# Layer 3's scores with both batches on the partitions, and every weighted sum over 256 columns in quarters

## The chip, the cores and the metric

The kernel runs on one core of one Trainium2 chip. The metric is the device time of one execution in microseconds. Most executions agree within 0.3%.

## What is computed

Four graph layers run on `x`, 32 batches of 512 nodes with 64 features, over one graph `adj` of 512 x 512. Each layer takes `h = max(layernorm(x), 0)` and adds its result to `x`.

```python
# layer 0: three steps of  v = W2 relu(W1 [v, adj v] + b1) + b2
# layer 1: two steps of    z = relu((adj z) W_i)
# layer 2: 8 heads and then one output head of
s = einsum('bnd,bmd->bnm', h, h) * graph
s = where(s == 0.0, -1e16, s)
a = softmax(s, axis=2)
out = einsum('bnm,bmd->bnd', a, h) + b          # h = x @ W
# layer 3: adj with ones on its diagonal
h = x @ weight
e = leaky_relu((h @ a[:D])[:, :, None] + (h @ a[D:])[:, None, :], 0.2)
h_prime = einsum('bij,bjd->bid', softmax(adj * e), h)
return h_prime + bias
```

So each pair of batches needs 16 score matrices of layer 2's heads, two of its output head and two of layer 3, all of 512 x 512 in float32.

## The kernel before

Batches go in 16 pairs, the two batches of a pair side by side. A *unit* is a set of scores in a tile `sm` of 128 partitions x 8 slots x 512 columns, taken from a ring of three such tiles. There are ten units for a pair: eight heads (`Heads`, each with 512 nodes in two parts of 64 partitions), the output head (`Out`), which holds 64 nodes of batch 0 in partitions 0 to 63 and 64 nodes of batch 1 in the others, and layer 3 (`Last`). In `Last` before, slots 0 to 3 belong to batch 0 and slots 4 to 7 to batch 1, with 128 nodes on the partitions.

A unit goes through steps. `scores` makes two slots at a time: TensorE for heads and `Out` (line 422, and line 425 adds the mask), and for `Last` one product for each batch of a repeated vector with the features `h3T` (line 690) and then ScalarE's Prelu with the source term `src` as bias (line 692). `maxima` multiplies a slot by the graph and takes its maximum on VectorE (line 443); the negated maxima are made on GpSimd (line 450). `exponentials` is ScalarE (line 454), `normalise` is a reciprocal on VectorE (line 464) and the scaling on GpSimd (line 466), `turn` transposes blocks of 32 x 32 on VectorE (line 472).

After the turn, the weighted sum over neighbours runs on TensorE in tiles of 32 rows x 64 columns. For each of 16 blocks of neighbours (`jb`) it takes products of the node features in quarters (`vq`) with the turned scores. A sum of two heads (`Two`, line 482) has eight products of 256 columns in a block, in both halves of the array's columns. `Ends` (line 750) sums the output head of one pair together with layer 3 of the pair before it: four products of 256 columns for the first, and eight of 128 columns for the second, four for each batch. The last three sums of the program, one of `Out` and two of `Last`, stand alone. Each float32 product shows as two instructions.

A sum lies in the four banks of the tag `mm`; the scores have four banks of their own, of the tag `s`. `evict` copies a finished sum to SBUF, to a tile of the tag `us`, of which there are two. For heads, line 516 reads it, and line 527 writes the activated result `y`; for `Ends`, lines 769 and 771 write it and line 588 turns it.

`quarters` (line 288) spreads node features over four groups of 32 partitions with 16 DMAs on SP's queue. It is called for the heads' values (`z`, two batches), the output head's (`hn`) and layer 3's (`h3n`, both batches in a row, line 671). `Out.chain` makes layer 3's inputs: `oA`, `oB`, `oC` are the layer norm, `oT` the transposed features, `oW` the product with the weight (line 649), `oN` the node features and source terms (lines 660, 668 and 669) and their quarters.

The order of all this on the engines is written out by hand. A step is a job with a tick and a place in it (`PLACES`); there are ten ticks a pair, and one sorted list of jobs gives the order of the instructions on each engine's queue. The letters are: `s` scores, `r` maxima, `x` exponentials, `n` normalise, `t` turn, `v` the parts of a weighted sum, `us` or `eu` the eviction, `w` and `y` the heads' weights, `o` and `c` the projection, `f` and `h` the output head's features and nodes, `F0` to `F24` the steps of layers 0 and 1 for the next pair. The units of the last stretch have an order of their own, `TAIL`. A sum is placed in two halves, `vA` and `vB`.

Of the kernel before, what the change touches and what calls it, by code (L numbers as in the profile page):

```python
# [21 lines left out]
def gnn_stack_kernel(  # L22
# [79 lines left out]
    A = const.tile([P, NT, N], F32, name="A")  # L102
# [3 lines left out]
    ones = const.tile([P, P], F32, name="ones")  # L106
    ivt = const.tile([1, 2, D], F32, name="ivt")
    W1n = const.tile([P, 2, P], F32, name="W1n")
    W2n = const.tile([P, P], F32, name="W2n")
# [8 lines left out]
    rows = const.tile([NB, P], F32, name="rows")  # L118
# [31 lines left out]
    nc.sync.dma_start(out=Wo_sb, in_=W_out.rearrange("(h d) o -> d h o", d=HID))  # L150

# [6 lines left out]
    b2rep = const.tile([P, P], F32, name="b2rep")  # L158
# [8 lines left out]
    A3 = A  # L167
    a2rep = const.tile([P, 2, P], F32, name="a2rep")
# [35 lines left out]
    def masks():  # L204

        for k in range(2):
            nc.vector.tensor_tensor(II[:, k, :], ident[:, 0:D], ident[:, D:P], ALU.add)
        nc.vector.tensor_copy(I2b, II[:, 0, :])

        nc.vector.tensor_scalar(NEGM, A, 0.0, NEG_INF, ALU.is_equal, ALU.mult)  # L210

        for t in range(NT):
            nc.gpsimd.affine_select(
                out=A3[:, t, blk(t)],
                in_=A[:, t, blk(t)],
                pattern=[[-1, P]],
                compare_op=ALU.not_equal,
                fill=1.0,
                base=0,
                channel_multiplier=1,  # L220
            )
# [5 lines left out]
    def grams():  # L227

        WT = hp.tile([P, H, D], F32, tag="us", name="WT")
# [10 lines left out]
    def vectors():  # L240
        for j in range(2):
            nc.vector.tensor_scalar(a2rep[:, j, :], ones, a2bd[:, j : j + 1], None, ALU.mult)
# [3 lines left out]
        w3T = hp.tile([P, P], F32, tag="us", name="w3T")  # L246
# [158 lines left out]
    class Unit:  # L405
# [68 lines left out]
        def weigh(self, part):  # L474
# [3 lines left out]
            for jb in range(part * JB // 2, (part + 1) * JB // 2):  # L478
# [21 lines left out]
    class Two(Unit):  # L500
# [30 lines left out]
        def stages(self):  # L531

            def evict():
                self.us = hp.tile([P, 4, N // 2], F32, tag="us", name="us")
# [36 lines left out]
            def nodes():  # L571
                s = state[self.p]
                pn = turned(s["HH"][self.j])
                hn = hp.tile([P, NT, D], F32, tag="hn", bufs=1, name="hn")
# [15 lines left out]

    def to_nodes(yT):
        return turned(yT).rearrange("p (t j d) -> p t j d", t=NT, j=2)

    class Out(Unit):
# [12 lines left out]
        def stages(self):  # L607
            s = state[self.p]

            def evict():  # L610

                self.yT = hp.tile([P, N], F32, tag="us", name="yT")
# [21 lines left out]
        def chain(self):  # L634
# [18 lines left out]
            def nodes():  # L653
                s["h3n"] = hp.tile([P, NT, 2, D], F32, tag="h3n", bufs=1, name="h3n")
                s["src"] = st.tile([P, NT, 2], F32, tag="src", name="src")
                for c in range(2):
# [12 lines left out]
                    nc.vector.tensor_copy(s["src"][:, 2 * c : 2 * c + 2], pn[:, :, P:])  # L669
# [8 lines left out]
    class Last(Unit):  # L678
# [5 lines left out]
        def scores(self, k):  # L684
            s = state[self.p]
            j = k // 2
            if k == 0:
                self.pd = [ps_s.tile([P, N], F32, tag="s", name="pd") for _ in range(2)]
                for pd, r, n in zip(self.pd, R, range(2)):
                    nc.tensor.matmul(pd, lhsT=a2rep[r, n, :], rhs=s["h3T"][r, :], start=True, stop=True)  # L690
            for i in range(2 * k, 2 * k + 2):
                nc.scalar.activation(
                    self.sm[:, i, :], self.pd[j], AF.Prelu, bias=s["src"][:, i % NT, j : j + 1], alpha=0.2
                )

        def maxima(self, i):
            self.by_graph(i, self.sm[:, i, :], A3[:, i % NT, :])
# [3 lines left out]
        def weighed(self, i, c):  # L701
            return state[self.p]["h3Q"][c], self.sm[:, c * NT : (c + 1) * NT, :]

        def stages(self):
            s = state[self.p]

            def evict():
                self.yT = hp.tile([P, N], F32, tag="us", name="yT")
                yT = self.yT.rearrange("p (t k i e) -> p k i t e", k=2, i=2, e=32)
                for i in range(4):  # L710
                    nc.scalar.activation(
                        yT[:, i // 2, i % 2],
                        self.u[i][:, 0:P].rearrange("p (t e) -> p t e", e=32),
# [4 lines left out]
            def residual():  # L718
                pn = to_nodes(self.yT)
                xo = xp.tile([P, NT, 2, D], F32, tag="xo", bufs=1, name="xo")  # L720
                nc.vector.tensor_tensor(xo, pn, s["x3"], ALU.add)
                for j in range(2):
                    nc.sync.dma_start(
# [6 lines left out]
    class Ends(Unit):  # L730
# [6 lines left out]


        def weigh(self, part):
            if part == 0:  # L740
                self.u = [mm_ps() for _ in range(4)]
            for jb in range(part * JB // 2, (part + 1) * JB // 2):
# [298 lines left out]
```

## Time and profile before

| | |
|---|---|
| median of 3 runs | 2349.54 us (2346.86 to 2351.03) |
| the profiled execution | 2346.53 us |
| its span, first to last instruction | 2344.7 us |
| mean granted TensorE clock | 0.977 |
| ScalarE's exponentials, line 454 | 912.2 us busy, 1280 of them |
| GpSimd's scaling, line 466 | 882.6 us busy, 1280 |
| VectorE's transposes, line 472 | 776.6 us busy, 640 |
| VectorE's maxima of heads and `Out`, line 443 | 733.0 us busy, 1152 |
| TensorE's sums of two heads, line 482 | 488.1 us busy |
| TensorE's joint sums, line 750 | 131.4 us busy |

Busy times of TensorE are unions over instructions that run side by side in several tiles of the array. "Idle before" in a row is the time for which the engine had nothing to run just ahead of the instruction, with what ended it behind the arrow. SPq is the queue on which SP issues DMAs, PEld TensorE's weight loads.

### The profile page before, as it was taken

Reading aid. Unit: us, or ns where it says so; the run is one execution under the profiler, and the core shown is the slowest. Engines: PE = TensorE matmul, PEld = TensorE weight load, DVE = VectorE, ACT = ScalarE, POOL = GpSimd, SP = SyncE. Lnnn points to the kernel's source line nnn. Section 1 sums busy time; section 2 is a strip of 40 time slices with the busy share of each in tenths; the row PEclk is TensorE's granted clock in tenths of the full one; section 3 lists DMA queues with packets and bytes.
Section 4 is the critical chain, followed back from the end, with each engine's and each line's share of the span. In section 5 each row is a group of like instructions: output and inputs, shape, how many; then the busy total and the mean of one; then the engine's idle time right before and its main releaser. Section 6 shows DMA issues by size and latency. Waiting matters only on the chain.

```text
span 2344.7 us, 81823 instructions
## 1 busy us (share of the span) xinstructions
PE 2189.2 (93%) x34507; PEld 1186.5 (51%) x34507; DVE 1872.8 (80%) x4098; ACT 1496.4 (64%) x3752; POOL 1306.7 (56%) x2163
## 2 busy tenths in 40 slices
PE   6889999999999999999999999999999999999883
PEld 3335555555555555555555555555555555554452
DVE  3558788888887888888888888888888888888654
ACT  1346557667676766767676676767667676766644
POOL 2345465655665565566656556665655666555433
PEclk9899999999999999999999999999999999999986
DMA  3001111202121120212112021211202121120112
GB/s 85 10 15 20 24 20 24 42 13 40 20 41 25 22 43 13 40 20 41 25 25 42 12 40 21 41 25 24 42 13 40 20 36 25 24 38 13 28 25 46
DMA packets 260596, 68.25 MB, mean 29 GB/s; under 512 B 257660, under 2 KB 258692, under 8 KB 260228
## 3 DMA queue, kind: packets, MB, share of 16 engines
q1 hardware_dynamic: 259424, 62.86, 15.9%
q8 instruction: 270, 4.42, 0.8%
q14 instruction: 98, 0.80, 0.1%
q10 hardware_dynamic: 804, 0.17, 0.0%
HBM read 8.40 MB, written 4.19 MB: 5 GB/s over the span
## 4 chain that ended last, share of the span: by engine, by line
PE 76%; DVE 10%; ACT 6%; POOL 3%; issue 2%; SPq 2%; DMA 1%; ACTq 0%; POOLq 0%; DVEq 0%
PE s L422 19%; PE mm L482 16%; PE mm L312 11%; PE mm L750 5%; PE mm L545 5%; PE s L425 4%; PE mm L516 4%; DVE sm L443 4%; DVE sm L472 4%; ACT sm L454 3%; PE mm L324 3%; PE mm L798 2%; SPq L294 2%; PE mm L358 2%; ACT y L527 1%
## 5 line engine op out<-in xcount | busy, mean ns | idle before, releaser
L454 ACT ACTIVATE sm<-sm,nmx 128x512 f32<-128x512 f32 x1280 | 912.2, 720 | 204.9 <-POOL nmx L450 198.0
L466 POOL TENSOR_SCALAR sm<-sm,rs 128x512 f32<-128x512 f32 x1280 | 882.6, 707 | 183.8 <-DVE rs L464 173.9
L472 DVE STREAM_TRANSPOSE sm<-sm 128x1024 f32<-128x1024 f32 x640 | 776.6, 1229 | 99.3 <-POOL sm L466 94.4
L443 DVE CUSTOM_DVE_ANT_0 sm<-s,A 128x512 f32<-128x512 f32 x1152 | 733.0, 680 | 139.1 <-PE s L425 131.7
L422 PE MATMUL s<-ZZ,Y 64*64 64x512 f32 x4096 | 572.0, 604 | 20.7 <-DVE mx L443 13.2
L482 PE MATMUL mm<-sm,vq 32*64 32x256 f32 (+1 forms) x17152 | 488.1, 378 | 29.8 <-DVE sm L472 20.3
L450 POOL TENSOR_SCALAR nmx<-mx 128x2 f32<-128x2 f32 x640 | 143.0, 229 | 608.5 <-DVE mx L443 550.8
L482 PEld LDWEIGHTS mm<-sm,vq 32*64 32x64 f32 x17152 | 400.3, 135 | 129.3 <-issue 56.6
L422 PEld LDWEIGHTS s<-ZZ,Y 64*64 64x64 f32 x4096 | 149.9, 132 | 254.0 <-issue 124.8
L425 PE MATMUL s<-NEGM,I2b 64*64 64x512 bf16 x2304 | 259.4, 378 | 0.0
L454 ACT ACTIVATION_READ_ACCUMULATOR sm<-sm,nmx 128x1 f32 x1280 | 250.1, 195 | 0.0
L537 ACT COPY us<-mm 128x256 f32<-128x256 f32 x256 | 75.9, 380 | 182.5 <-PE mm L482 182.5
L312 PE MATMUL mm<-AT,v 128*128 128x512 f32 x384 | 172.9, 593 | 0.0
L527 ACT ACTIVATE y<-mm,cols 128x512 f32<-128x512 f32 x256 | 159.9, 686 | 9.1 <-PE mm L516 9.1
L425 PEld LDWEIGHTS <-I2b 64*64 64x64 bf16 x2304 | 81.1, 107 | 160.5 <-issue 160.4
L750 PE MATMUL mm<-sm,vq 32*64 32x128 f32 (+1 forms) x5504 | 131.4, 313 | 27.4 <-issue 21.5
L516 PE MATMUL mm<-us,Wh 64*64 64x512 f32 x1024 | 134.1, 595 | 17.4 <-ACT us L537 17.4
L272 POOL TENSOR_TENSOR r<-ve,mhalf 128x8 f32<-128x8 f32 x64 | 110.8, 1731 | 54.4 <-DVE ve L270 39.4
L750 PEld LDWEIGHTS mm<-sm,vq 32*64 32x64 f32 x5504 | 111.8, 132 | 52.7 <-issue 29.4
L263 POOL TENSOR_TENSOR xc<-x,nmu 128x512 f32<-128x512 f32 x48 | 55.3, 1151 | 139.8 <-DVE nmu L261 139.8
L545 PE MATMUL mm<-y,Wo_sb 128*64 128x512 f32 x512 | 125.2, 605 | 0.0
L312 PE MATMUL mm<-AT,z 128*128 128x512 f32 x256 | 119.1, 609 | 3.8 <-DVE z L276 1.4
(135 smaller groups left out, 1979.0 us busy)
## 6 DMA issues: line engine op xcount, KB each, us to landing
vq<-z SPq DMA_DIRECT2D x512, 32.0 KB, 1.9
vq<-hn SPq DMA_DIRECT2D x512, 32.0 KB, 1.9
vq<-h3n SPq DMA_DIRECT2D x512, 32.0 KB, 1.9
xt<-in_x_dram SPq DMA_DIRECT2D x32, 128.0 KB, 2.4
out_dram<-xo SPq DMA_DIRECT2D x32, 128.0 KB, 2.0
A<-in_adj_dram SPq DMA_DIRECT2D x3, 1024.0 KB
Wh<-in_L_gnn_Wh_dram SPq DMA_DIRECT2D x2, 256.0 KB
Wo_sb<-in_L_gnn_W_out_dram SPq DMA_DIRECT2D x1, 256.0 KB
```

The costliest lines, as they stand in the source:

```text
L312: nc.tensor.matmul(pe, lhsT=v[:, m].rearrange("p j d -> p (j d)"), rhs=AT[:, m, :], start=(first and m == 0), stop=(m == NT - 1),)
L422: nc.tensor.matmul(pss[half][R[ab], :], lhsT=lhsT, rhs=rhs, start=True, stop=False)
L425: nc.tensor.matmul(pss[half][R[ab], :], lhsT=I2b[R[half], :], rhs=NEGM[R[half], k, :], start=False, stop=True,)
L443: nc.vector.tensor_tensor_reduce(self.sm[:, s, :], src, graph, 1.0, -FMAX, ALU.mult, ALU.max, self.mx[:, s : s + 1])
L454: nc.scalar.activation(self.sm[:, s, :], self.sm[:, s, :], AF.Exp, bias=self.nmx[:, s : s + 1], accum_out=self.ssum[:, s : s + 1],)
L466: nc.gpsimd.tensor_scalar(self.sm[:, s, :], self.sm[:, s, :], self.rs[:, s : s + 1], 1.0, ALU.mult, ALU.mult)
L472: nc.vector.transpose(out=two, in_=two)
L482: nc.tensor.matmul(self.u[i][R[c], 0 : weights.shape[1] * 32], lhsT=values[32 * i : 32 * i + 32, jb, :], rhs=weights[32 * i : 32 * i + 32, ...
L516: nc.tensor.matmul(py[c][r, :], lhsT=Wh2[R[c], 2 * (self.q - 1 + c) + ab, r], rhs=self.us[R[c], 2 * ab : 2 * ab + 2].rearrange("p i (s e) ...
L527: nc.scalar.activation(y, py[c], AF.Prelu, bias=cols[:, h : h + 1], alpha=0.01)
L545: nc.tensor.matmul(pa[R[ab], :], lhsT=Wo_sb[:, h, :], rhs=self.y[h], start=(k == 0), stop=(k == 1),)
L750: nc.tensor.matmul(self.u[i][R[c], (s % NS) * 32 : (s + ns) * 32], lhsT=values(i)[r, jb, :], rhs=sm[r, s : s + ns, 32 * jb : 32 * jb + 32] ...
```

## The change

Layer 3's unit takes the form of the output head's: a slot has 64 nodes, of batch 0 on partitions 0 to 63 and of batch 1 on the others. One product makes its scores for both batches. The graph for it, `A3`, is a tile of its own with 64 nodes twice on the partitions, loaded from `adj` by two more DMAs of 1 MB and given ones on its diagonal by 16 selections in the first pair. The source terms, which line 669 leaves with 128 nodes on the partitions, are moved to the new form by four DMAs in a pair. The joint sum has 256 columns in each product. All sums are placed in four quarters, `vA` to `vD`. The tag `us` has one buffer, `hn` and `h3n` share one, and tiles that only the start needs (`A`, `W1n`, `W2n`, `ones`, `rows`, `b2rep`) lie in the places of later ones. `PLACES` and `TAIL` are new throughout.

```diff
-    A = const.tile([P, NT, N], F32, name="A")
+    A = ap_.tile([P, NT, N], F32, tag="sm", name="A")
+    A3 = const.tile([P, NS, N], F32, name="A3")
...
-    ones = const.tile([P, P], F32, name="ones")
-    W1n = const.tile([P, 2, P], F32, name="W1n")
-    W2n = const.tile([P, P], F32, name="W2n")
+    early1 = hp.tile([P, 4, P], F32, tag="h3T", bufs=1, name="early1")
+    W1n, W2n, ones = early1[:, 0:2], early1[:, 2], early1[:, 3]
+    early2 = hp.tile([P, 2, P], F32, tag="h3n", bufs=1, name="early2")
...
     nc.sync.dma_start(out=Wo_sb, in_=W_out.rearrange("(h d) o -> d h o", d=HID))
+    for r in R:
+        nc.sync.dma_start(out=A3[r], in_=adj.rearrange("(s q) m -> q s m", q=D))
...
-        for t in range(NT):
-            nc.gpsimd.affine_select(
-                out=A3[:, t, blk(t)],
...
+    def loops():
+        for s in range(NS):
+            for base in (0, -D):
+                nc.gpsimd.affine_select(
+                    out=A3[:, s, hblk(s)],
+                    in_=A3[:, s, hblk(s)],
...
         def weigh(self, part):
-            for jb in range(part * JB // 2, (part + 1) * JB // 2):
+            for jb in range(part * JB // 4, (part + 1) * JB // 4):
...
-                self.us = hp.tile([P, 4, N // 2], F32, tag="us", name="us")
+                self.us = hp.tile([P, 4, N // 2], F32, tag="us", bufs=1, name="us")
...
-                hn = hp.tile([P, NT, D], F32, tag="hn", bufs=1, name="hn")
+                hn = hp.tile([P, NT, D], F32, tag="h3n", bufs=1, name="hn")
...
-                    nc.vector.tensor_copy(s["src"][:, 2 * c : 2 * c + 2], pn[:, :, P:])
+                    nc.vector.tensor_copy(src[:, 2 * c : 2 * c + 2], pn[:, :, P:])
+                s["src"] = st.tile([P, NS], F32, tag="src", bufs=2, name="src")
+                for j in range(2):
+                    for h in range(2):
+                        nc.sync.dma_start(
+                            out=s["src"][R[j]].rearrange("r (t h) -> r t h", h=2)[:, :, h], in_=src[R[h], :, j]
+                        )
                 tag = "h3Q" if self.p < NPAIR - 1 else "hQ"
                 s["h3Q"] = [quarters(s["h3n"][:, :, j, :], f"{tag}{j}") for j in range(2)]
...
             if k == 0:
-                self.pd = [ps_s.tile([P, N], F32, tag="s", name="pd") for _ in range(2)]
-                for pd, r, n in zip(self.pd, R, range(2)):
-                    nc.tensor.matmul(pd, lhsT=a2rep[r, n, :], rhs=s["h3T"][r, :], start=True, stop=True)
+                self.pd = ps_s.tile([P, N], F32, tag="s", name="pd")
+                nc.tensor.matmul(self.pd, lhsT=a2rep, rhs=s["h3T"], start=True, stop=True)
...
     class Ends(Unit):
         def weigh(self, part):
-            for jb in range(part * JB // 2, (part + 1) * JB // 2):
-                tiles = [(0, 0, NS, lambda i: state[self.attn.p]["hQ"][i // 2], self.attn.sm)]
-                if self.last:
-                    for j in range(2):
-                        tiles.append((1, j * NT, NT, lambda i, j=j: state[self.last.p]["h3Q"][j], self.last.sm))
...
+            units = [(state[self.attn.p]["hQ"], self.attn.sm)]
+            if self.last:
+                units.append((state[self.last.p]["h3Q"], self.last.sm))
+            for jb in range(part * JB // 4, (part + 1) * JB // 4):
+                for (values, sm), r in zip(units, R):
                     for i in range(4):
+                        q = slice(32 * i, 32 * i + 32)
                         nc.tensor.matmul(
+                            self.u[i][r, 0 : N // 2],
+                            lhsT=values[i // 2][q, jb, :],
+                            rhs=sm[q, :, 32 * jb : 32 * jb + 32],
+                            start=(jb == 0),
+                            stop=(jb == JB - 1),
                         )
...
-        for part, half in enumerate("AB"):
-            at(t, f"v{half}{k}", lambda part=part: unit.weigh(part))
+        for part, quarter in enumerate("ABCD"):
+            at(t, f"v{quarter}{k}", lambda part=part: unit.weigh(part))
...
+        if p == 0:
+            at(base, "A3", loops)
```

## The prediction

> **What bounds the kernel now.** I read the page first, then a table of busy time over one steady pair of batches, then TensorE's instructions in order of time around one sum of layer 2's attention and layer 3, the other engines there, and last the chain at the end.
>
> ```profile
> PE 2189.2 (93%) x34507; PEld 1186.5 (51%) x34507; DVE 1872.8 (80%) x4098; ACT 1496.4 (64%) x3752; POOL 1306.7 (56%) x2163
> ...
> PE 76%; DVE 10%; ACT 6%; POOL 3%; issue 2%; SPq 2%; DMA 1%; ACTq 0%; POOLq 0%; DVEq 0%
> ...
> 1105.90:1242.30 136.40, 133.19 (x2144) 71.96 (x2144) 116.55 (x256) 93.36 (x235) 81.63 (x134) 1.00 0.17 29
> ```
>
> The third line is one pair, columns as on the page (PE, PEld, DVE, ACT, POOL, clock, DMA share, GB/s). TensorE is busy 133.2 of 136.4 us, VectorE 116.6. Sums of this kind begin at 421.4, 558.6 and so on to 2062.7 us: 13 periods of about 136.8 us. A steady pair is TensorE's own length.
>
> ```profile
> 1105.94 4.67 PE L750 MATMUL mm<-sm,vq 32*64 32x256 f32 x201 [0.28 <-DVE sm L472]
> 1111.18 2.66 PE L750 MATMUL mm<-sm,vq 32*64 32x128 f32 x128 [0.57 <-issue]
> 1114.66 1.38 PE L750 MATMUL mm<-sm,vq 32*64 32x128 f32 x55 [0.82 <-issue]
> 1115.97 1.09 PE L422 MATMUL s<-ZZ,Y 64*64 64x512 f32 x8
> ...
> 1134.38 7.16 PE L482 MATMUL mm<-sm,vq 32*64 32x256 f32 x256
> 1141.47 1.09 PE L422 MATMUL s<-ZZ,Y 64*64 64x512 f32 x8
> ...
> 1225.54 1.09 PE L516 MATMUL mm<-us,Wh 64*64 64x512 f32 x8 [1.30 <-ACT us L537]
> ```
>
> The joint sum (line 750) holds TensorE from 1105.94 to 1115.97, 10.03 us, with two gaps that wait for nothing; a sum of two heads (line 482), which weighs as many score columns, takes 7.09 us. Besides these, one steady pair has only waits of 1.30 and 0.28 us on TensorE.
>
> ```profile
> 1113.37 2.58 DVE L472 STREAM_TRANSPOSE sm<-sm 128x1024 f32<-128x1024 f32 x2 [0.21 <-POOL sm L466]
> 1117.30 0.69 DVE L443 CUSTOM_DVE_ANT_0 sm<-s,A 128x512 f32<-128x512 f32 x1 [1.35 <-PE s L425]
> ...
> 1212.36 0.78 ACT L668 COPY h3n<-mm 128x256 f32<-128x256 f32 x2
> 1213.16 18.94 SPq L294 DMA_DIRECT2D vq<-h3n  x28
> 1214.71 4.73 ACT L692 ACTIVATE sm<-pd,src 128x512 f32<-128x512 f32 x8 [1.57 <-PE pd L690]
> ...
> 2307.81 0.65 ACT L668 COPY h3n<-mm 128x256 f32<-128x256 f32 x2 [6.19 <-DMA vq<-h3n]
> ```
>
> VectorE waits 1.35 us for scores after the joint sum: it is that little ahead there. SP issues a DMA each 0.64 us. In the tail that issuing is the chain: node features are copied at 2307.81 only when the earlier ones' 32 DMAs have read their tile.
>
> **What the skill says.** The Trainium skill, "TensorE: Matmul & The Clock Gate", Part 3, says that a weight load overlaps a running product only where the row group differs. That fits the slow joint sum: per block of 32 neighbours each row group gets three products of 256, 128 and 128 columns, against two of 256; line 312 streams a pass of 512 columns in 427 ns (eight in 3.43 us of the chain), so 256 take 213 and 128 only 107, below the 132 ns of a weight load in the trace. "TensorEngine Tiling (Array Packing)", Key Properties, says that a change of tile shape drains the array; 7.09 us against 32 passes of 213 ns (6.82) leaves 0.27 us for going in and out. "DMA: Bandwidth & Descriptors", Why a DMA increments its semaphore by 16 and not by 1, says that a descriptor moves one contiguous run: each new source DMA, 64 partitions by 4 separate floats, is 256 descriptors of 4 bytes. No steady transfer here has that form; the quarters' 128 runs of 256 bytes land 1.9 us after issue.
>
> **Part by part**, against the profiled execution's 2346.5 us (span 2344.7, some 1.8 around it; 3.0 below the median of 2349.5).
>
> 1. *Joint sum.* Two 128-column products of each row group become one of 256; with layer 3 in the form of a sum of two heads I take 7.09 us. The 13 steady sums took 9.84 to 11.72 us, mean 10.33: 3.24 us off each, 42.1 us of TensorE's time. The first, without layer 3 (7.62 us), stays.
> What arrives of it? Let T be the end of the last transpose before the sum. The new order still puts the rest of head 4 ahead of the first maximum of head 5: four maxima (0.61 us each), two reciprocals, eight scalings on GpSimd (0.685 each) and four transposes (1.2 each). Maxima end at T+2.5; the last exponentials at T+5.2; then one reciprocal and, in order, four transposes, to T+10.1. TensorE would have filled the four score banks by T+9.6, and gets its next bank at T+10.7 and the rest one by one: scores end at T+13.2, where they ended at T+15.45 before. So 2.25 us arrive, and 13 x 2.25 = 29.3 us. Ends of this term: 0 if VectorE is late by more elsewhere, 42.1 if its work was ahead.
>
> 2. *Layer 3's scores.* One product over 128 partitions for two over 64: 1.06 us becomes 0.85 (two passes at 427 ns, as line 312's eight in 3.43 us). 14 times 0.2 is -2.8. The eight Prelu and eight maxima keep size and count.
>
> 3. *Quarters.* I put the old and new places in order: on TensorE all four quarters stand together in 66 of the 82 sums, as the halves did in all; only the sum of heads 4 and 5 is split, by one score group, once a pair. 16 x 0.27 = +4.3 us. Its bounds: 0 (the group drains anyway) to twice that.
>
> 4. *Source terms by DMA.* Four DMAs a pair on SP ahead of the 32 of the quarters, so these start 4 x 0.64 = 2.6 us later; they had 5.6 us to spare (SP's order in time has the last issue end at 1234.7, landing 1.9 after its start, the sum at 1242.35), and the moved step below adds more. Landing: copy on VectorE 0.8 us after the product of line 660, three issues (1.9), landing 1.9: 4.6 us after that product. The new order puts the second half-step of layer 0 (lines 358 and 312, 4.45 us on TensorE) between it and the score product, so Prelu could not begin before 5.6 us. Hidden by 1 us. Behind the waiting Prelu on ACT stand six exponentials and the copies of `us` that TensorE already awaits for 1.30 us. I take that wait as unchanged: its bounds are 0 and 2.3. Uncovered, the source term costs 2.5 us a pair, 35 in all.
>
> 5. *The tail.* Its joint sum, on the chain (2257.97 to 2268.04), loses 3.0. But node features pass twice through SP's queue, each time now behind four DMAs and VectorE's copy: 2 x (2.6 + 0.4) = +6.0. Net +3.0. Bounds -3 and +9, as the tail's order is written anew.
>
> 6. *Costed at nothing.* One buffer for `us`: sums follow 24 us apart, and the last reader is done within 7 us of the copy; without that cover ACT waits for line 516. `hn` in `h3n`'s tile: the 16 DMAs end about 1203, the next copy is at 1212.4; the new order leaves 18 us of TensorE's work between instead of 24, so some 4 us of cover. The second 2 MB of graph: issued behind `Wo_sb` (26 us), as long as the 16 us of the first (chain, 15.15 to 31.3), done before the next quarters at 71.6. 16 selections instead of 4 (288 ns before) lie on GpSimd, 40% idle in a pair. Early tiles in later ones' places are read out before these are written. The head has 22.8 us of gaps between 60 and 300 us whose order changes: 0, with 6 either way.
>
> Sum: -29.3 - 2.8 + 4.3 + 3.0 = -24.8, so 2321.7 for such an execution and 2325 for the median.
>
> **Rivals.**
> *All of TensorE's saving arrives*: -42.1 - 2.8 + 4.3 + 3.0 = -37.6, 2312; with the 1.30 us wait gone in 13 pairs too, 2295. For it: VectorE's 116.6 of 133 us leaves room. Against: its chain of POOL and transposes after the joint sum.
> *VectorE takes the bound*: each pair then keeps some 136 us and only the tail and head move, about 2344 (2338 to 2352). For it: VectorE was 1.35 us ahead and TensorE's wait for it (0.28) is there already. Against: 20 us idle a pair.
> *Slower: the 4-byte DMAs are late.* Place: the first Prelu of layer 3, with exponentials and `us` behind it. With landing L, Prelu is late by L - 2.9 us. From L of about 5 us the 2.25 of a pair are gone; at 8 us it is 14 x 5.1 = 71 lost, against 25 won: 2396. For it: no 4-byte transfer of steady state in the trace, one such load in the head landed after 13.1 us. Against: that one stood behind megabytes of graph; 4 KB is little.
> *The change doesn't do what it says*: quarters that TensorE runs back to back are halves. True mostly, and priced so in 3.
>
> **How the numbers follow.** Chances: forecast 0.47 (2325, its own range 2314 to 2336), all arrives 0.30, VectorE bound 0.12, late DMAs 0.11. 0.2% is what a measurement of this kernel can tell from no change, so same is 2345 to 2354. Faster: 0.47 + 0.30 + 0.07 = 0.84; same 0.05; slower 0.11. The range 2300 to 2346 leaves out the late DMAs and the low end of the first rival.
>
> **What would show it.** Line 750's successor: 256 instructions in one 32x256 form, 7.1 us start to next start, no gaps for issue; a pair near 134.5 us (133.3 if all arrives, 136.5 if VectorE binds); VectorE without its 1.35 us wait and TensorE waiting for maxima after the joint sum; the first Prelu waiting for the score product, not for a DMA; the tail some 3 us longer after the last steady sum. A wait of ACT for the `src` DMA, or for `h3n`, in each pair would prove me wrong.

## The result and the profile after

The changed kernel takes 2333.36 us (median of four runs, 2331.5 to 2338.17) against 2349.72 us, a ratio of 0.9935 with a 95% interval of 0.9918 to 0.9953: 16.4 us faster, where 24.7 were forecast. The profiled execution took 2338.17 us (span 2336.3), the longest of the four; that of the kernel before took 2346.53, less than any of its timed runs. So the two traces differ by only 8.4 us.

Lines of the kernel have moved by about five: the joint sum is now line 756 (750 before), a sum of two heads 487 (482), scores 427 and 430 (422, 425), layer 3's score product 697 (690), keys 804 (798), the heads' weights 521 (516), Prelu 699 (692), the copies of `us` 542 (537), exponentials 459 (454), transposes 477 (472), maxima 448 (443).

The page of the changed kernel, the engines' busy times and the shares of the chain that ended last:

```profile
PE 2186.7 (94%) x32683; PEld 1172.3 (50%) x32683; DVE 1857.4 (80%) x4100; ACT 1493.1 (64%) x3752; POOL 1299.6 (56%) x2175
...
PE 76%; ACT 9%; DVE 6%; POOL 2%; SPq 2%; issue 1%; DMA 1%; ACTq 0%; DVEq 0%; POOLq 0%
```

The table of one steady pair of it, from one joint sum to the next (columns as before):

```profile
1098.93:1234.41 135.48, 132.82 (x2015) 71.05 (x2014) 115.59 (x256) 93.00 (x236) 80.92 (x134) 1.00 0.18 29
```

TensorE runs 1824 matmuls and as many weight loads fewer, and "issue" falls from 2% to 1% of the chain. But a pair is only 1.4 us shorter, where 2.2 were forecast.

TensorE of the changed kernel in order of time, in that pair:

```profile
1098.93 7.90 PE L756 MATMUL mm<-sm,vq 32*64 32x256 f32 x256
1106.77 1.09 PE L427 MATMUL s<-ZZ,Y 64*64 64x512 f32 x8
...
1120.32 1.09 PE L427 MATMUL s<-ZZ,Y 64*64 64x512 f32 x8 [0.69 <-ACT Y L814]
...
1207.78 7.59 PE L487 MATMUL mm<-sm,vq 32*64 32x256 f32 x256
...
1218.32 1.09 PE L521 MATMUL mm<-us,Wh 64*64 64x512 f32 x8 [1.72 <-ACT us L542]
```

The joint sum is one form without a gap, 7.84 us from its start to the next score product. Yet two waits are longer or new: 0.69 us for `Y`, which was not there, and 1.72 us for `us` instead of 1.30. A third kind shows only in the length of the first block of a sum. The sums at 1098.93 and 1207.78 take 7.8 and 7.5 us instead of 7.09, because one of the four `mm` banks that they need is still held by a step of layers 0 and 1: the fourth product of the first waits for ScalarE's `z` (line 385), that of the second for VectorE's addition of line 370. The second of these is new. The joint sum waited for a bank before, too: its first block took 0.92 us there, until VectorE's addition into `cat` (line 561) had read the bank.

VectorE ahead of the joint sum and after it, and ScalarE ahead of the `us` copies, in the same trace:

```profile
1097.66 1.20 DVE L477 STREAM_TRANSPOSE sm<-sm 128x1024 f32<-128x1024 f32 x1
...
1105.71 2.48 DVE L477 STREAM_TRANSPOSE sm<-sm 128x1024 f32<-128x1024 f32 x2
1108.12 0.67 DVE L448 CUSTOM_DVE_ANT_0 sm<-s,A 128x512 f32<-128x512 f32 x1
...
1206.09 4.73 ACT L699 ACTIVATE sm<-pd,src 128x512 f32<-128x512 f32 x8 [0.68 <-DMA src<-src]
1213.40 0.72 ACT L459 ACTIVATE sm<-sm,nmx 128x512 f32<-128x512 f32 x1 [2.59 <-POOL nmx L455]
```

VectorE's wait of 1.35 us is gone, as foreseen. TensorE doesn't wait longer for VectorE after the sum, though. Four groups of scores follow in 5.14 us, exactly as long as before (1115.97 to 1121.11). The work behind these scores begins, in the changed kernel and then in the kernel before, at:

```profile
1111.91 1.09 PE L593 MATMUL mm<-ident,yT 128*128 128x128 f32 x8
```

```profile
1121.11 1.09 PE L588 MATMUL mm<-ident,yT 128*128 128x128 f32 x8
```

In both, the last two of the four groups come in pieces that the maxima release, 2.94 us instead of the 2.31 us of two groups that wait for nothing (1157.35 to 1159.66 before). And the Prelu does wait for the `src` DMAs.

Where a pair's TensorE time went: from each matmul to the next one's start, summed by kind over 12 steady pairs, us per pair.

| | before | after | |
|---|---|---|---|
| joint sum | 10.36 | 7.84 | -2.53 |
| score product of layer 3 | 1.06 | 0.94 | -0.12 |
| the four sums of two heads | 28.41 | 29.03 | +0.62 |
| keys, with the wait for `Y` behind them | 4.20 | 4.64 | +0.45 |
| masks, with the wait for `us` behind them | 11.61 | 11.62 | +0.02 |
| all others | 81.13 | 81.29 | +0.15 |
| a pair | 136.77 | 135.36 | -1.42 |

SP's queue in the tail of the changed kernel:

```profile
2273.39 2.64 SPq L676 DMA_DIRECT2D src<-src  x4
2276.13 20.66 SPq L299 DMA_DIRECT2D vq<-h3n  x32
2299.24 2.62 SPq L676 DMA_DIRECT2D src<-src  x4
```

The two times 2.6 us ahead of the quarters are there, as worked out. Against the trace before, 12 steady pairs give -17.0 us, the head +1.0, and all that follows the last steady joint sum +7.6.

### The profile page after: what moved, and what is told of

It is laid out like the page before. It is cut to its first block, busy times and chain, and to the rows that moved or that the text cites. A ratio compares the mean times of both kernels' runs of the same rounds, so it can differ in the third digit from the quotient of the medians.

```text
span 2336.3 us, 78517 instructions
## 1 busy us (share of the span) xinstructions
PE 2186.7 (94%) x32683; PEld 1172.3 (50%) x32683; DVE 1857.4 (80%) x4100; ACT 1493.1 (64%) x3752; POOL 1299.6 (56%) x2175
## 4 chain that ended last, share of the span: by engine, by line
PE 76%; ACT 9%; DVE 6%; POOL 2%; SPq 2%; issue 1%; DMA 1%; ACTq 0%; DVEq 0%; POOLq 0%
PE s L427 20%; PE mm L487 17%; PE mm L317 9%; ACT sm L459 6%; PE mm L550 5%; PE mm L756 5%; PE mm L521 5%; PE s L430 5%; DVE sm L477 4%; PE mm L329 3%; PE mm L804 3%; SPq L299 2%; PE mm L363 1%; DVE sm L448 1%; PE mm L593 1%
## 5 line engine op out<-in xcount | busy, mean ns | idle before, releaser
L471 POOL TENSOR_SCALAR sm<-sm,rs 128x512 f32<-128x512 f32 x1280 | 869.8, 699 | 149.1 <-DVE rs L469 109.0
L487 PE MATMUL mm<-sm,vq 32*64 32x256 f32 (+1 forms) x17152 | 502.7, 380 | 26.0 <-DVE sm L477 18.3
L455 POOL TENSOR_SCALAR nmx<-mx 128x2 f32<-128x2 f32 x640 | 148.3, 235 | 600.6 <-DVE mx L448 544.7
L487 PEld LDWEIGHTS mm<-sm,vq 32*64 32x64 f32 x17152 | 401.8, 135 | 141.7 <-issue 55.9
L756 PE MATMUL mm<-sm,vq 32*64 32x256 f32 x3712 | 118.0, 380 | 10.2 <-DVE sm L477 8.8
L317 PEld LDWEIGHTS mm<-AT,v 128*128 128x128 f32 x384 | 73.2, 191 | 93.3 <-issue 91.7
```

What stands on the lines that cost most here:

```text
L317: nc.tensor.matmul(pe, lhsT=v[:, m].rearrange("p j d -> p (j d)"), rhs=AT[:, m, :], start=(first and m == 0), stop=(m == NT - 1),)
L471: nc.gpsimd.tensor_scalar(self.sm[:, s, :], self.sm[:, s, :], self.rs[:, s : s + 1], 1.0, ALU.mult, ALU.mult)
L487: nc.tensor.matmul(self.u[i][R[c], 0 : weights.shape[1] * 32], lhsT=values[32 * i : 32 * i + 32, jb, :], rhs=weights[32 * i : 32 * i + 32, ...
L756: nc.tensor.matmul(self.u[i][r, 0 : N // 2], lhsT=values[i // 2][q, jb, :], rhs=sm[q, :, 32 * jb : 32 * jb + 32], start=(jb == 0), stop=(j ...
```

## Experiments

Kernels ran on several chips, on which the kernel before took 2348 to 2354 us, so they are compared by their ratio to it; that of the changed kernel is 0.9935. The 2354 us belong to two kernels alone, those with 0.9905 and 0.9901. Against the 2349 us of the others, their times would give 0.9925 and 0.9918, so the length of a pair, from the trace, is the safer measure there.

| | median us | ratio, 95% interval | steady pair, us |
|---|---|---|---|
| layer 3's joint products in two of 128 columns | 2369.24 | 1.0086 (1.0071 to 1.0101) | 138.15 |
| one of four head sums in 128 columns | 2435.62, one run | | 141.99 |
| old order, new layout | 2357.69 | 1.0040 (1.0026 to 1.0054) | 137.07 |
| five places moved | 2346.88 | 0.9989 (0.9981 to 0.9998) | 136.42 |
| two `src` DMAs as VectorE copies | 2343.29 | 0.9978 (0.9969 to 0.9986) | 136.49 |
| both of the last two | 2345.97 | 0.9989 (0.9982 to 0.9996) | 136.82 |
| `us` later by two copies | 2349.82 | 1.0007 (0.9998 to 1.0015) | 136.47 |
| a tile for the last `hn` | 2335.17 | 0.9943 (0.9929 to 0.9958) | 135.34 |
| `us` ahead of two exponentials | 2331.48 | 0.9905 (0.9888 to 0.9921) | 135.14 |
| that, the five places and the `hn` tile | 2329.82 | 0.9901 (0.9886 to 0.9916) | 135.09 |
| `cat` copied on ScalarE | 2345.09 | 0.9982 (0.9975 to 0.9988) | 136.33 |
| the last two together, and the tail's `src` on two queues | 2335.14 | 0.9936 (0.9922 to 0.9949) | 135.58 |

### Why was the joint sum slow?

The first kernel gives layer 3's products their old size and keeps everything else:

```diff
-                for (values, sm), r in zip(units, R):
+                for c, (values, sm) in enumerate(units):
+                    for a, b in ((0, NS),) if c == 0 else ((0, NT), (NT, NS)):
...
-                            self.u[i][r, 0 : N // 2],
+                                self.u[i][R[c], a * 32 : b * 32],
```

> The changed kernel with layer 3's part of the joint sum again in two products of 128 columns, so 24 products in a block instead of 16; layout and order stay. Theory A, instructions do not come fast enough: the joint sum grows from 7.8 us to 10 to 11 us, its blocks stay at 0.43 us each, the extra is two or three pauses of about 1 us that wait for nothing, each ending shortly after a 16 KB load of the instruction queue, and the kernel is 30 to 40 us slower than the changed one, about 2365 to 2375 us. Theory B, as predicted, a weight load that is longer than a 128-column pass: the sum grows as much, but evenly, to some 0.6 us a block. Theory C, the form of the sum was not the source of the gain: the time stays at 2333 us.

The second cuts the products of one sum of two heads in four in half, where layer 3 is not involved at all:

```diff
+                    cuts = ((0, NT), (NT, NS)) if getattr(self, "q", 0) == 1 and self.j == 0 else ((0, NS),)
+                    for a, b in cuts:
...
+                                rhs=weights[32 * i : 32 * i + 32, a:n, 32 * jb : 32 * jb + 32],
```

> The changed kernel with one of the four head sums of a pair (the first two heads) in products of 128 columns, so 32 products in a block instead of 16. Theory A, instructions arrive at about 75 a us (256 in 3.4 us in the trace of before): 2048 instructions of that sum with its weight loads take some 13.7 us instead of 7.1. Theory B, weight loads of 132 ns bound each row group (eight for its two passes of four products, 1.06 us a block, if they follow one another): some 17 us if none overlaps, about 8.5 us if the two column halves overlap, and evenly in all blocks. Theory C, neither: 7.1 us, since the streamed columns are the same.

TensorE in order of time, in the first of these kernels (joint sum, line 757):

```profile
1111.86 4.85 PE L757 MATMUL mm<-sm,vq 32*64 32x256 f32 x203
1117.75 2.66 PE L757 MATMUL mm<-sm,vq 32*64 32x128 f32 x128 [1.04 <-issue]
1121.77 1.37 PE L757 MATMUL mm<-sm,vq 32*64 32x128 f32 x53 [1.37 <-issue]
```

And in the second (a sum of two heads, line 490):

```profile
1089.91 3.56 PE L490 MATMUL mm<-sm,vq 32*64 32x128 f32 x203
1094.31 2.30 PE L490 MATMUL mm<-sm,vq 32*64 32x128 f32 x128 [0.83 <-issue]
1098.06 2.30 PE L490 MATMUL mm<-sm,vq 32*64 32x128 f32 x128 [1.45 <-issue]
1101.54 1.18 PE L490 MATMUL mm<-sm,vq 32*64 32x128 f32 x53 [1.18 <-issue]
```

Read the counts: between two pauses there are 128 matmuls, in both kernels and in the joint sum before (the x128 at 1111.18 there). With a weight load to each that is 256 instructions. The page lists 270 transfers of 4.42 MB on a queue of kind "instruction" for the kernel before, so 16,384 bytes each. In the trace before they start at 1108.98, 1112.33 and 1115.81 us, in the last kernel at 1091.89, 1095.47, 1099.34 and 1102.66, each of about 1 us: one in 3.3 to 3.9 us, and a pause ends 2.2 to 2.6 us after a load starts. In the changed kernel there are 256 loads, 14 fewer, about what its 3,648 fewer matmuls and weight loads fill. TensorE uses up 256 instructions faster than they come, some 66 to 77 a microsecond.

Inside a burst the blocks of neighbours show that nothing else is slow. Start of a block to the next, us:

```
before, 24 matmuls a block:         0.918 0.509 0.437 0.490 0.432 0.431 0.432 0.432 1.444 0.436 0.460 ...
after, 16 matmuls a block:          1.037 0.432 0.432 0.431 0.432 0.432 0.431 0.432 0.432 ...
heads in 128 columns, 32 a block:   0.487 0.561 0.503 0.462 0.555 0.443 1.686 0.556 0.445 0.511 2.238 ...
```

A block of 24 takes as long as one of 16, 0.43 us, and one of 32 takes 0.44 to 0.56: a weight load of 132 ns behind a product of 128 columns costs little. (The long first block is the wait for a bank, told above.) With 16 matmuls a block the demand is 32 instructions in 0.432 us, 74 a microsecond, which the supply just meets; 24 ask for 111. The whole sum in 128 columns took 12.5 to 14.5 us in the steady pairs instead of 7.09. That length lies in the ranges of two of the theories; the form decides it, bursts and pauses, not slow blocks. So theory A holds in both kernels: the cause is the supply of instructions. The first row of the table says that 36 us would be lost again by this one cut, more than the whole change gains.

### What does the new order do for the `src` DMAs?

The next kernel is the new layout in the old order of places: `vA` and `vB` at the old `vA`'s place, `vC` and `vD` at the old `vB`'s, `A3` as in the change.

> The new layout of layer 3, the new tiles and the source terms by DMA, but all steps in the order of the kernel before, with the first two quarters of a sum where its first half and second half began, back to back. Theory A, the predicted one: a steady pair is TensorE's length and gains some 2.3 to 2.9 us from the joint sum, but Prelu comes 2.5 us later, because nothing stands between the source terms and the scores; that pause and the wait for the us copies behind it leave a pair at 136 to 137 us and the kernel at 2345 to 2360 us. Theory B, the new order gave nothing: 2333 us or less. Theory C, the Prelu's delay is absorbed: a pair of 134 us, 2315 us.

ScalarE in order of time there:

```profile
803.76 0.78 ACT L670 COPY h3n<-mm 128x256 f32<-128x256 f32 x2
808.08 4.73 ACT L699 ACTIVATE sm<-pd,src 128x512 f32<-128x512 f32 x8 [3.54 <-DMA src<-src]
```

With nothing placed in between, the first Prelu waits 3.54 us for the source terms, and TensorE behind it 2.0 to 3.4 us for `us`. The ratio 1.0040 against 0.9935 says that the new places are worth about 25 us; the change without them would have been slower than the kernel before. (Some of the 25 is a lowered clock, see below.) Theory A fits, with a pair of 137.07 us.

### Are the new waits for banks and `Y` the missing time?

Five places were moved: two steps of layers 0 and 1 ahead, so that they free their banks before the sums, the output head's nodes behind the keys, and the split sum joined.

```diff
-"h0": (5, 51)   "F13": (4, 73)   "F18": (6, 107)   "vC3": (1, 227)     "vD3": (1, 245)
+"h0": (4, 323)  "F13": (4, 43)   "F18": (6, 67)    "vC3": (1, 219.3)   "vD3": (1, 219.6)
```

> The changed kernel with five places moved: the step of layer 1 that uses a sum bank goes ahead of a score group before the joint sum; the residual of layer 0 goes ahead of layer 3's first maximum; the output head's nodes go between keys and scores; the last two quarters of the split sum follow the others. Theory A, these places make the new waits of TensorE (0.6 us at the joint sum and 0.4 at the sum after layer 3's scores for a bank, 0.7 for the keys, 0.2 for the split): a pair falls from 135.4 to 133.6 us, the kernel to about 2312 us. Theory B, VectorE bounds a pair: the waits reappear elsewhere as waits for maxima, the kernel stays within 5 us of 2333.

Neither: it is 13 us slower than the changed kernel. The waits are gone at the sums of two heads (-0.55 us a pair) and behind the keys (-0.76), and shorter at the joint sum (-0.26; its first block still takes 0.77 us, for the same bank). But TensorE now comes to the weights earlier and waits 2.15 us for `us`. Line 521 in order of time, then the same stretch as a table:

```profile
1085.79 1.97 PE L521 MATMUL mm<-us,Wh 64*64 64x512 f32 x8 [2.15 <-ACT us L542]
1087.52 1.91 PE L427 MATMUL s<-HH 64*64 64x512 f32 x8
...
1090.33 1.04 PE L427 MATMUL s<-HH 64*64 64x512 f32 x8
```

```profile
1086.00:1090.00 4.00, 4.00 (x28) 0.59 0.32 52
1090.00:1095.00 5.00, 5.00 (x52) 1.00 0.33 54
```

The columns are TensorE's busy time and the granted clock. Eight products take 1.97 us instead of 1.09; after some 4 us they are back at 1.04. Pairs with such a stretch last 136.7 us, pairs without it 135.05. So the loss is the clock, and even without it the pair gains 0.3 us, not the 1.6 that the three terms add up to; where the rest went stays open.

Two kernels were to test that the pause is what lowers the clock. One makes `us` late in the changed kernel, by two more copies ahead of it in that one sum:

```diff
-                for i in range(4):
+                extra = (0, 0) if self.j == 0 and self.q == NQ - 1 else ()
+                for i in (*extra, 0, 1, 2, 3):
                     nc.scalar.copy(self.us[:, i], self.u[i][:, 0 : N // 2])
```

> The changed kernel with the first of the four copies of `us` done three times instead of once, in the one sum of a pair for whose eviction TensorE waits 1.72 us (the second sum of batch 0): ScalarE gives `us` 0.58 us later, and nothing else changes. Theory A (a TensorE pause of over 2 us lowers the granted clock): the pause becomes 2.3 us, most pairs get a stretch of about 4 us at half clock, and the time grows by 12 x 0.58 = 7 us for the wait and by 10 to 12 times 1.7 us for the clock: 2355 to 2362 us. Theory B (the clock has nothing to do with the pause): 2338 to 2343 us. Theory C (the wait is hidden or made up later in the pair): 2331 to 2336 us.

TensorE in order of time where the pause had this effect, and the table there and at a pause that had none:

```profile
1361.12 1.98 PE L521 MATMUL mm<-us,Wh 64*64 64x512 f32 x8 [2.54 <-ACT us L543]
```

```profile
1357.13:1360.54 3.41, 1.45 (x17) 1.00 0.26 43
1360.54:1363.96 3.42, 2.84 (x16) 0.50 0.30 48
...
537.93:541.34 3.41, 2.35 (x54) 1.00 0.26 44
541.34:544.76 3.42, 1.94 (x20) 1.00 0.34 55
544.76:548.17 3.41, 3.41 (x44) 1.00 0.31 50
```

The pause grew to 2.54 us, and a stretch of half clock followed 4 of the 13, not most of them. Pairs lasted 136.1 us without it and 137.5 with it. The mechanism of theory A is shown, its frequency was overrated. What decides is where the pause lies. In all 14 traces the granted clock changes only at steps of a grid of 3.41 us; the rows are windows of that grid. The pause before 1361.12 leaves TensorE idle for 1.96 us of one window, and the next window runs at 0.50. The pause before 542.82, as long, is cut by a boundary into 1.06 and 1.48 us, and the clock stays at 1.00. The other kernel, which was to shorten the pause, is told next.

### Do the `src` DMAs lengthen the wait for `us`?

```diff
-                    for h in range(2):
-                        nc.sync.dma_start(
-                            out=s["src"][R[j]].rearrange("r (t h) -> r t h", h=2)[:, :, h], in_=src[R[h], :, j]
-                        )
+                    to = s["src"][R[j]].rearrange("r (t h) -> r t h", h=2)
+                    nc.vector.tensor_copy(to[:, :, j], src[R[j], :, j])
+                    nc.sync.dma_start(out=to[:, :, 1 - j], in_=src[R[1 - j], :, j])
```

> The changed kernel with two of the four `src` DMAs of a pair replaced by two VectorE copies (the halves that stay on their partitions); the other two DMAs and everything else as they are. In the changed kernel the Prelus of layer 3 wait 0.4 to 0.7 us a pair for the `src` DMAs (0.68 us in the median), and the eviction of `us`, and with it TensorE's wait of 1.72 us for it, stand behind them on ScalarE. Theory A (the `src` DMAs lengthen that wait): the Prelus start about 0.5 us earlier, TensorE's wait falls to 1.1 to 1.3 us, 12 x 0.5 = 6 us and in the tail two times 1.3 us: 2322 to 2328 us. Theory B (the exponentials behind the Prelus wait for the maxima of VectorE, which the two new copies delay): wait unchanged, 2331 to 2336 us, only the tail gains.

> The kernel with the five moved places of the earlier run (2346.88 us; there TensorE waits 2.15 us a pair for `us`, and after ten of the twelve waits the granted clock was 0.5 for about 4 us, which costs 1.7 us each: pairs of 135.05 us without and of 136.7 us with it), with the `src` DMAs cut from four to two as in the other run of this call. Theory A (a TensorE pause of over 2 us is what lowers the granted clock; pauses of 1.7 us never did in the changed kernel): the pause falls below 2 us, the lowered stretches go, and the pairs fall to about 134.6 us: 2346.9 - 17 - 6 = 2322 to 2328 us. Theory B (the lowered clock comes of the order, not of the pause's length): pairs of 136.2 us or more, 2340 to 2345 us.

Of the four DMAs, the two whose halves stay on their partitions become copies on VectorE. The second kernel has the five moved places as well. (In the trace of the five places half clock followed nine of the 13 pauses, not ten of twelve.)

With two DMAs the Prelu waits for the score product (0.17 us) and no longer for a DMA, and the wait for `us` is 1.72 us as before: theory B, as far as this wait goes. But a pair became 1.13 us longer, which neither foresaw. VectorE of the first of these kernels, in order of time:

```profile
1206.36 0.98 DVE L676 COPY src<-src 64x4 f32<-64x4 f32 x2
1207.37 4.62 DVE L477 STREAM_TRANSPOSE sm<-sm 128x1024 f32<-128x1024 f32 x4
...
1212.50 0.68 DVE L370 TENSOR_TENSOR x<-xt,mm 128x512 f32<-128x512 f32 x1
```

The two copies hold VectorE for 1.0 us, four transposes stand behind them, and behind these the addition of line 370, which frees the bank that the next sum waits for; TensorE waits there 0.94 us. In the kernel with both edits the pause for `us` rose to 2.33 us instead of falling below 2. A likely reason is that what ScalarE waits for comes through VectorE: its waits for the negated maxima grew from 203.9 to 221.5 us over the 12 pairs. Half clock followed 4 of its 13 pauses. So the premise of theory A of that run failed, and this run alone can't tell it from theory B.

### The wait for `us` itself

In the changed kernel TensorE ends the sum at 1079.8 us and the scores behind it at 1081.1, but ScalarE runs two exponentials of layer 3 until 1082.2 and only then copies `us`. One place moves these two behind the copies; the second kernel adds the five places and a tile of its own for the last pair's second `hn`.

```diff
-        "x3e": (0, 258)
+        "x3e": (0, 282.5)
```

> The changed kernel with one place moved: the last two of the six exponentials of layer 3 that stand on ScalarE between the sum's last product and the copies of `us` come after these copies. In the changed kernel TensorE ends that sum at 1081.1 us, ScalarE runs two exponentials until 1082.2 and copies `us` then, and TensorE waits 1.72 us. Theory A (that queueing on ScalarE is most of the wait): the wait falls to about 0.7 us, 12 x 1.0 = 12 us: 2319 to 2325 us. Theory B (the exponentials that are put off are late next, or VectorE's chain of transposes and maxima sets the pair's length): 2330 to 2336 us.

> The five moved places of the earlier run, the exponentials of the other run of this call put behind `us`, and the last pair's second `hn` in a tile of its own. Theory A (in the five places' run only the longer wait for `us`, 2.15 us, and the lowered clock behind it ate the gain of 1.5 us a pair on the `mm` banks, the keys and the halves): with the wait at about 0.7 us no lowered clock, pairs of 133.5 to 134 us, 2305 to 2316 us. Theory B (the pair's length is set by another engine, so that what the moves save comes back as a wait elsewhere): pairs of 135 us or more, 2326 to 2335 us.

TensorE's waits over the steady pairs (total, times, longest, us), in the changed kernel and then in the one with the exponentials moved:

```profile
PE mm L521 <- ACT us L542: 20.6, 12, 1.7
PE s L427 <- ACT Y L814: 8.3, 12, 0.7
```

```profile
PE s L427 <- ACT Y L814: 8.3, 12, 0.7
PE mm L756 <- DVE sm L477: 4.2, 13, 0.3
PE mm L521 <- ACT us L542: 3.7, 12, 0.3
```

The wait went from 1.72 to 0.31 us, and the pair shortened by 0.22 us only. Set side by side, the 12 pairs of each kernel show where the rest came back. TensorE gains 1.41 us ahead of the weights and 0.28 in the joint sum; it loses 0.64 us in the scores and keys right behind the weights, 0.39 ahead of the joint sum, where it now waits for VectorE's transposes (the 4.2 us above), 0.33 in the scores after that sum and 0.15 in the projection. Theory B in both kernels. The combined kernel has the shortest time of all, but 135.09 us a pair again.

### Which engine sets the pair now?

Three orders with different TensorE waits gave 135.05 to 135.14 us, the first of them in its pairs at full clock. To see whether VectorE is behind it, the copy into `cat` went to ScalarE. The second kernel adds this to the combined one, and changes the tail: two of the four `src` DMAs of each of the last two units on ScalarE's queue, and a tile of its own for the last `h3n`.

```diff
-                    nc.vector.tensor_copy(s["cat"], pa)
+                    nc.scalar.copy(s["cat"], pa)
```

> The changed kernel with one kind of work moved from VectorE to ScalarE: the copy of the first projection into `cat` (two of 0.69 us a pair). Theory A (VectorE's chain sets the length of a pair now: added VectorE work of 1.15 us lengthened a pair by 1.13 us, and three orders with different TensorE waits all end at 135.05 to 135.15 us): the pair shortens by one or both copies, 0.6 to 1.3 us, 12 pairs: 2317 to 2327 us, ratio to the kernel before 0.986 to 0.990. Theory B (TensorE with its waits for ScalarE sets it): the pair is unchanged or a little longer for ScalarE's new work, 2331 to 2338 us, ratio 0.992 to 0.995.

> The combined kernel of the last call (pairs of 135.09 us, ratio 0.9901) with the `cat` copies on ScalarE, and in the last two units of layer 3 two of the four `src` DMAs issued from ScalarE's queue and the last `h3n` in a tile of its own. Theory A (VectorE sets the pair): pairs of 133.8 to 134.5 us and a tail shorter by 3 to 4 us: ratio 0.980 to 0.986, some 2303 to 2317 us beside a kernel before of 2350 us. Theory B (it does not): pairs of 135.0 us or more, only the tail gains: ratio 0.987 to 0.990.

Theory A falls, and theory B has the direction but not the size: the pair grew by 0.97 us on average (0.6 to 0.7 in most pairs; one of 139.1 us holds a pause of 3.23 us and half clock), and by 0.49 in the combined kernel. The new tail gained nothing: from the last steady joint sum to the end it takes 285.3 us, and 285.4 in the combined kernel. VectorE with less to do, in order of time:

```profile
1205.74 2.34 DVE L477 STREAM_TRANSPOSE sm<-sm 128x1024 f32<-128x1024 f32 x2
1209.10 0.18 DVE L469 RECIPROCAL rs<-ssum 128x4 f32<-128x4 f32 x1 [1.02 <-ACT sm L459]
1209.84 0.43 DVE L671 COPY src<-mm 128x4 f32<-128x4 f32 x2 [0.56 <-ACT h3n L670]
```

Its reciprocal waits 1.02 us for exponentials that the copy has put off on ScalarE; in the changed kernel it didn't wait there. Then come the four transposes and the same bank, whose sum takes 0.64 us longer. So in that stretch work on ScalarE and work on VectorE both lengthen the pair: the two `src` copies of 0.98 us by 1.13, the later `us` copies, a pause 0.82 us longer, by 0.74 at full clock. The chain runs from ScalarE's exponentials over VectorE's transposes to the bank of TensorE's next sum.

### The tail

```diff
+                own = self.p == NPAIR - 1 and self.j == 0
-                hn = hp.tile([P, NT, D], F32, tag="h3n", bufs=1, name="hn")
+                hn = hp.tile([P, NT, D], F32, tag="h3T" if own else "h3n", bufs=1, name="hn")
```

> The changed kernel in which the second `hn` of the last pair has a tile of its own (the tile of `h3T`, free then) instead of the one that it shares with the first `hn`. In the changed kernel this copy waits 5.86 us on ScalarE for the quarter DMAs of the first `hn`, six exponentials of layer 2 stand behind it, and TensorE idles 8.8 us ahead of the last joint sum. Theory A (that queueing is the growth of the last pair from 195.3 to 201.0 us): the wait goes, the joint sum ends about 5 us earlier and so does all that follows: 2327 to 2329.5 us. Theory B (SyncE's queue of 32 quarters, which ends at 2258 us, holds the tail anyway): 2331 to 2335 us.

ScalarE's wait of 5.86 us is gone, yet the ratio, 0.9943, is not below 0.9935: theory B. The last joint sum in order of time, in the changed kernel and here:

```profile
2247.63 8.57 PE L756 MATMUL mm<-sm,vq 32*64 32x256 f32 x248 [8.80 <-DVE sm L477]
```

```profile
2242.64 8.67 PE L757 MATMUL mm<-sm,vq 32*64 32x256 f32 x256 [8.79 <-DVE rs L469]
```

TensorE idles as long as before. That this trace has the sum 5 us earlier is not the tile's doing: in the kernel with only the two exponentials moved it starts at 2240.86. The trace of the changed kernel has a sum at half clock there, while the kernel with the exponentials moved runs it at full clock (tables of the stretch, the changed kernel first):

```profile
2183.50:2190.00 6.50, 6.47 (x122) 4.40 (x122) 0.00 (x0) 0.00 (x0) 2.25 (x4) 0.53 0.09 16
```

```profile
2180.00:2187.00 7.00, 6.68 (x182) 3.83 (x190) 0.64 (x3) 1.18 (x4) 2.89 (x5) 1.00 0.10 16
```

A block takes 0.86 us there instead of 0.43. That would fit the profiled execution, the longest of its four, which also has their lowest mean clock (0.976 against 0.978 to 0.980); the other three have no trace. The last pair is 201.0 us in it, 196.9 in the other, 195.3 before. So of the 7.6 us about 4 are the change's own, an estimate from one trace of each kernel.

## Why the prediction was right, and where it was not

*The joint sum (step 1)* was right in what it becomes and wrong in why. It is one form, and behind the first block its blocks of 0.43 us are those of a sum of two heads. The forecast put the old length down to weight loads of 132 ns behind passes of 107 ns, with the rule of the Trainium skill, "TensorE: Matmul & The Clock Gate", Part 3, that a load overlaps a running product only where the row group differs. The blocks don't show that: 24 matmuls take the 0.43 us of 16, though each row group then has six loads of 132 ns, 0.79 us in all. Here the measurement decides against the rule as it was used. The pauses are the supply of 256 instructions at a time. That the size came out nearly the same is luck: both causes go away with fewer instructions.

*What arrives of it* failed as put. Foreseen were 3.24 us off the sum, of which VectorE would let 2.25 through. VectorE held TensorE after the sum no longer than before. All of the shorter sum arrived, as the first rival had it, but it was 2.53 us shorter. The 7.09 us left out the wait for a bank that the joint sum had before and has now: it adds 0.56 us to the first block and 0.19 to the last. The time T + 13.2 for the end of the scores came out, T + 13.05 (1098.86 to 1111.91), because two errors cancel: the sum is 0.75 us longer than put, the scores behind it nearly 1 us shorter. (For the kernel before, T + 15.45 should read T + 15.2, from 1105.89 to 1121.11.)

*The score product (step 2)* gave 0.12 us a pair instead of 0.2, *the split sum (step 3)* cost 0.19 instead of 0.27 (two halves of 3.64 us against 7.09).

*The source terms (step 4)*: issue and landing were nearly right (2.6 to 2.9 us for the four and 1.9 us), but the cover was said to have 1 us to spare and was 0.7 us short, in 12 pairs of 12. The term that was too small is the one ahead of them, 0.8 us from the product to the end of VectorE's copy: in the pair shown the product of line 662 ends at 1200.39 and the copy, which waits for ScalarE's `h3n`, at 1202.45, so 2.1 us. What stands behind the Prelu mattered less than feared, for the exponentials there wait for maxima anyway: without the DMA wait the wait for `us` stayed. The rival of late 4-byte DMAs had the right place, and the old order shows its price, but a landing of 1.9 us, not 5, kept it out.

*Not in the sum at all* were waits that the new places made: the bank at the sum of two heads behind layer 3's first scores (+0.43 us a pair), `Y` (+0.45 with the keys). Per pair: forecast -2.25 - 0.20 + 0.27 = -2.18; measured -1.42. The difference of 0.76 is -0.28 for the joint sum, +0.08 and -0.08 for steps 2 and 3, +0.43 and +0.45 for these waits, and +0.16 for the rest. Over 12 pairs that is 9 us, the size of the miss.

*The tail (step 5)*: +3.0 forecast, about +4 once the half clock of that one trace is set aside, +7.6 with it.

What stays open: which single chain ends a pair at 135.1 us. Added work on TensorE, ScalarE and VectorE each lengthened it nearly in full, and waits removed from TensorE came back elsewhere. In the combined kernel the sum behind line 370 takes 7.09 us and waits for nothing, so there the chain through that bank isn't the one. A kernel with less work on ScalarE and VectorE together, or with other places for the transposes ahead of that bank, was not tried.

## What to carry to other kernels

A gap on TensorE that waits for nothing, every 128 float32 matmuls with a weight load each, pointed here to too many small products: count instructions per microsecond before blaming the weight loads. When a hand-written order is nearly balanced, price a shorter step by what the next engine in turn will do, and look in the new order for who holds the PSUM banks of the step that comes earlier. Keep TensorE's waits well below 2 us: a wait that grows a little can nearly double its cost through the clock.

## What had not been expected of the hardware

*Instructions come in loads of 16,384 bytes, one in 3.3 to 3.9 us* while TensorE outruns them: bursts of 128 matmuls with their 128 weight loads, then a pause of 0.6 to 1.5 us. The 66 to 77 instructions a microsecond just fed the products of 256 columns here and starved those of 128.

*A short pause can halve TensorE's clock.* No pause of 1.72 us at the weights was followed by a lower clock (12 or 13 each in the changed kernel and in those with the `src` copies, the `hn` tile and 128 columns). Of pauses of 2.0 to 3.4 us there, 9 of 13 were in the kernel with five places, 10 of 13 in the old order, 4 of 13 in each of the two others. The clock is then 0.50 for one window of 3.41 us, which costs 1.4 to 1.7 us. What counts is TensorE's idle time within one window of that grid. Over the steady pairs of all 14 traces, all 27 windows with 1.86 us or more of it were followed by one at half clock, one of the five with 1.76 to 1.83 us was, and none of the 6,637 with less. The Trainium skill, "TensorE: Matmul & The Clock Gate", Part 1, has the half clock after an idle window of about 3.4 us that runs freely. The traces agree with free windows of 3.41 us. They don't agree that a window has to be idle throughout: some 1.8 us were enough, so the measured bound is the one to use.

*A DMA of 256 separate 4-byte elements* landed 1.9 us after its issue, no later than 128 runs of 256 bytes.
